# A four-layer graph network on one core: layer 0's weight products from 7 block products instead of 8, with a planner that prefers open PSUM banks

## The chip, the cores and the metric

The kernel runs on one core of a Trainium2 chip. Its engines are TensorE (PE in the profile, with its weight loads as PEld), VectorE (DVE), ScalarE (ACT), GpSimd (POOL) and SyncE (SP), which here only issues DMA transfers. The metric is the device time of one execution in microseconds (us); shorter is better. A profiled execution also has a span, from its first to its last instruction, which is a little shorter than its device time.

## What is computed

`x` is (64, 256, 128): 64 batches, 256 nodes, 128 channels. `adj` is (256, 256). Everything is fp32. Cut to what matters:

```python
def layernorm(x, eps=1e-5):                       # over the 128 channels, no gain, no bias
    return (x - mean(x)) / sqrt(var(x) + eps)

# layer 0: six propagations, adj twice, three powers each; seven 128x128 weights
xs = [x, A@x, A@A@x, A@A@A@x, A@x, A@A@x, A@A@A@x]
x = layernorm(x + sum(xs[k] @ W[:, :, k] for k in range(7)))
# layer 1
x = layernorm(x + A @ (x @ w1) + b1)
# layer 2: Ahat = A + I, scaled by its row sums d**-0.5 on both sides
x = layernorm(x + (Anorm @ x) @ W2.T + b2)
# layer 3: five steps of a gated unit
h = x
for _ in range(5):
    av = concat(A @ h, A @ h)
    u3 = h @ u3_w.T + u3_b
    z = sigmoid(av @ w3_w.T + w3_b + u3)
    r = sigmoid(av @ w4_w.T + w4_b + u3)
    hv = tanh(av @ w5_w.T + w5_b + (r * h) @ u5_w.T + u5_b)
    h = (1 - z) * h + z * hv
x = layernorm(x + h)
```

In layer 0 the two adjacencies are the same, so equal powers share one weight: with `w0s[0] = W0 + I` (the residual) and `w0s[k] = Wk + W(k+3)`, and with each weight's mean over the output channels taken off so that the result is already centred, the layer is `x w_0 + A x w_1 + q w_2 + A q w_3`, where `q = A A x`. The kernel forms `s = (x w_0 + q w_2) + A (x w_1 + q w_3)`.

## The kernel before

**Groups.** The batches go two at a time (`NB` = 2), which makes 32 groups. A group's data is a tile of 128 partitions by 512 columns: two batches, two halves of the 256 nodes, 128 channels. Each group goes through the four layers; up to `ACTIVE` = 10 groups are under way at once (`gate`, `load_gate`).

**Planner.** Nothing is issued as it is written. Each group records its steps (`Group.record`) as operations with an engine, a planned cost, a lag after it, the values it reads and writes, and a rank (the group's number; for the last 7 groups compressed so that they advance together). `Plan.order` (L84) then lays all operations out by list scheduling: at each turn it takes, for each engine, the operation that could start first, and among those of equal start the one of lowest rank and then of lowest record number (L117). A value gets a buffer ("slot") when its first operation is placed and gives it back after its last user; the eight PSUM banks are such slots. The order that comes out is the program: each engine executes its own list in that order, and a semaphore holds an instruction until what it needs is there.

**Products by seven blocks.** `Group.seven` (L593) multiplies a 256x256 adjacency with a group's data as a 2x2 block matrix in the manner of Strassen and Winograd: 7 products of 128x128 blocks, with sums of blocks made on POOL (`ts01`, `ts2`, `ts3`) and put together on ACT and DVE. Its PE work is four operations: `first` (1 block product, L626), `middle` (3, which need the sums, L629), `more` (1, L634) and `rest` (2, L637). `more` overwrites a part of the bank that ACT must have copied before (`kept`, L655), and `rest` overwrites parts that the DVE operations `post12` and `post13` must have read.

**Layer 0.** For groups from the fifth batch on ("far" groups, 30 of 32) `x` is turned by a DVE transpose of 32x32 blocks, a DMA write to memory and two DMA reads (L745 to L755); its channels arrive in an order of their own, so the kernel holds a copy of two weights permuted to match (`w0p`, made by four DMAs, L308). `q` comes from `seven`. Then, for each node half `t`, four matmuls 128 to 256 columns wide make `x [w_0 w_1]` and `q [w_2 w_3]` side by side into one bank (`first`, L764, tiles `py`), ACT copies the right half out as `v` (L771), two matmuls per half add `A v` to the left half (`second`, L777), and ACT copies the sum out as `s0` (L783). Two banks are held for it.

**Layer norm.** `spread_of` (L509): four ACT squares with a running sum (L515) leave the variances in `ve`; POOL adds eps (L519) and takes the power -1/2 (L520).

**Start and end.** Constants are loaded and prepared first, with ranks that place them among the first groups' work: `p_an`, the transposes of the normalised adjacency (L259, L344), which need `ahat` scaled by DVE (L334); `p_w2u3T` and `p_w435u5T`, the turned weights of layers 2 and 3 (L391). The last three groups (`END` = 6 batches) end in `closing` (L557), which turns `h` back and centres it on PE; the others go back through a transpose and DMAs.

The line of every matmul in the profile is that of the helper `mm` (L199), so they are told apart by their tiles: `py` weight products and layer 0, `pm` and `pmq` and `pmg` the block products of layers 1 and 2, of `q`, and of layer 3, `pr` and `ph` the gates. An fp32 matmul or weight load shows as two instructions.

## Time and profile before

| what | value |
|---|---|
| device time, median of 4 runs | 1353.43 us (1350.84 to 1355.65) |
| the profiled execution: device time | 1350.84 us |
| the profiled execution: span | 1348.9 us |
| mean granted TensorE clock | 0.999 |
| ACT busy | 758.1 us, 56% of the span |
| POOL busy | 680.7 us, 50% |
| DMA engines, mean busy share of the main queue | 34.1% |

The profiled execution was the fastest of the four; 1.9 us of its time lie outside the span. A row of the profile's groups names the source line, the engine, the operation, the tiles written and read, the shape and the count, then the busy time and the mean duration of one; a row of the timeline gives the start and the duration in us. Matmuls are pipelined, so that a matmul's duration in such a row is longer than the distance to the next one's start; it is the distance between starts that says what a matmul costs PE.

### The profile page before, as it was taken

The page shows a single profiled execution, that of the slowest core. Times are in us where ns is not written, and L with a number is a line of the kernel's source. Part 1 is how long each engine was busy: PE and PEld are TensorE (multiplying, and loading weights), DVE is VectorE, ACT ScalarE, POOL GpSimd, SP SyncE. Part 2 cuts the span into 40 slices and gives each one's busy share as a digit, 9 for nine tenths or more (in the row PEclk, how much of TensorE's full clock was granted, in tenths as well). Part 3 has the DMA queues.
Part 4 walks back from the last instruction along what each step waited for, and adds up shares of the span by engine and source line. Part 5 has one row for each costly group of instructions (what it writes and reads, how often), then busy time and mean ns, then how long its engine had stood idle before and what let it go on. Part 6 is the DMA issues. An engine that isn't in the chain of part 4 may idle for free.

```text
span 1348.9 us, 22012 instructions
## 1 busy us (share of the span) xinstructions
PE 1335.8 (99%) x6553; PEld 927.7 (69%) x6553; DVE 940.2 (70%) x2304; ACT 758.1 (56%) x2421; POOL 680.7 (50%) x1097
## 2 busy tenths in 40 slices
PE   8999999999999999999999999999999999999997
PEld 7986656677766666677666666676776776565554
DVE  5466677767667667865676776676666677777776
ACT  4675536467554566546565554474655686444445
POOL 5885425276742566247366443382653686233323
PEclk9999999999999999999999999999999999999999
DMA  6322334242422333433233433341332223333323
GB/s 180 107 69 80 90 93 129 75 130 87 134 78 79 109 95 118 122 103 96 63 113 107 133 98 97 95 134 56 113 99 63 83 85 122 86 104 95 95 77 110
DMA packets 269496, 134.96 MB, mean 100 GB/s; under 512 B 175777, under 2 KB 241057, under 8 KB 269377
## 3 DMA queue, kind: packets, MB, share of 16 engines
q1 hardware_dynamic: 269120, 133.42, 34.1%
q8 instruction: 53, 0.87, 0.3%
q14 instruction: 67, 0.54, 0.1%
q0 software_dynamic: 256, 0.13, 0.1%
HBM read 67.31 MB, written 65.80 MB: 99 GB/s over the span
## 4 chain that ended last, share of the span: by engine, by line
PE 97%; DMA 1%; DVE 1%; ACT 1%; issue 0%; POOLq 0%; SPq 0%; ACTq 0%; POOL 0%; DVEq 0%
PE pr L199 31%; PE ph L199 20%; PE pmg L199 19%; PE py L199 16%; PE pm L199 7%; PE pmq L199 4%; DMA w_raw<-in_L_gnn_weight_dram 0%; PE s L199 0%; DMA x<-in_x_dram 0%; ACT y L515 0%; ACT y L551 0%; DVE s L543 0%; POOLq L908 0%; DVE w0s L289 0%; PE p_an L259 0%
## 5 line engine op out<-in xcount | busy, mean ns | idle before, releaser
L199 PE MATMUL pr<-mg,w435u5T 128*128 128x512 f32 x640 | 319.8, 593 | 0.0
L614 POOL TENSOR_TENSOR tsg<-h 128x256 f32<-128x256 f32 x128 | 96.9, 758 | 291.0 <-DMA h<-dh 207.6
L722 ACT ACTIVATE r<-pr,bsum 128x512 f32<-128x512 f32 x160 | 109.7, 685 | 152.2 <-PE pr L199 151.7
L722 ACT ACTIVATE pr<-pr,bsum 128x512 f32<-128x512 f32 x160 | 105.5, 660 | 112.4 <-PE pr L199 111.4
L729 DVE TENSOR_TENSOR rh<-r,hT 128x512 f32<-128x512 f32 x160 | 122.4, 765 | 61.8 <-ACT r L722 60.9
L199 PE MATMUL ph<-rh,w435u5T 128*128 128x512 f32 x320 | 163.6, 594 | 0.0
L199 PE MATMUL ph<-mg,w435u5T 128*128 128x512 f32 x320 | 163.3, 592 | 0.0
L199 PE MATMUL pr<-hT,w2u3T 128*128 128x512 f32 x320 | 163.0, 593 | 0.0
L729 DVE TENSOR_TENSOR d<-ph,hT 128x512 f32<-128x512 f32 x160 | 109.7, 686 | 76.3 <-ACT ph L722 73.4
L199 PEld LDWEIGHTS pr<-mg,w435u5T 128*128 128x128 f32 x640 | 109.4, 191 | 65.3 <-issue 53.8
L722 ACT ACTIVATE ph<-ph,bsum 128x512 f32<-128x512 f32 x160 | 105.6, 660 | 60.4 <-PE ph L199 59.9
L531 ACT ACTIVATE y<-s,rs 128x128 f32<-128x128 f32 x384 | 122.1, 393 | 10.3 <-POOL rs L520 10.0
L515 ACT ACTIVATE y<-s 128x128 f32<-128x128 f32 x396 | 116.7, 300 | 17.1 <-DVE s L538 15.1
L199 PEld LDWEIGHTS pmg<-s_aTp,tsg 128*128 128x128 f32 x768 | 101.8, 192 | 33.5 <-issue 29.6
L652 DVE TENSOR_TENSOR mg<-pmg,usg 128x256 f32<-128x256 f32 x160 | 67.0, 420 | 72.1 <-PE pmg L199 69.8
L199 PEld LDWEIGHTS pmg<-aTp,h 128*128 128x128 f32 x512 | 87.1, 197 | 39.4 <-issue 29.2
L729 DVE TENSOR_TENSOR pr<-pr,d 128x512 f32<-128x512 f32 x157 | 108.7, 692 | 1.5
L520 POOL TENSOR_TENSOR rs<-ve,half 128x4 f32<-128x4 f32 x99 | 103.6, 1046 | 8.3
L519 POOL TENSOR_SCALAR ve<-ve 128x4 f32<-128x4 f32 x99 | 23.7, 240 | 165.6 <-ACT y L515 165.2
L729 DVE TENSOR_TENSOR hT<-hT,pr 128x512 f32<-128x512 f32 x157 | 106.1, 676 | 1.3
L199 PE MATMUL pmg<-s_aTp,tsg 128*128 128x128 f32 x768 | 106.2, 275 | 0.0
L642 DVE TENSOR_TENSOR usg<-usg,pmg 128x128 f32<-128x128 f32 x160 | 45.2, 284 | 83.2 <-PE pmg L199 48.0
(181 smaller groups left out, 2815.7 us busy)
## 6 DMA issues: line engine op xcount, KB each, us to landing
dh<-th SPq DMA_DIRECT2D x160, 256.0 KB, 2.0
h<-dh SPq DMA_DIRECT2D x256, 128.0 KB, 2.5
x<-in_x_dram SPq DMA_DIRECT2D x32, 256.0 KB, 3.4
hT<-dh SPq DMA_DIRECT2D x128, 64.0 KB, 2.0
out_dram<-y SPq DMA_DIRECT2D x32, 256.0 KB, 2.3
dx<-tx SPq DMA_DIRECT2D x30, 256.0 KB, 2.4
xT<-dx SPq DMA_DIRECT2D x60, 128.0 KB, 2.6
dn<-tn SPq DMA_DIRECT2D x29, 256.0 KB, 2.0
```

The lines of the kernel that those rows point to most:

```text
L199: nc.tensor.matmul(o, lhsT, rhs, start=start, stop=stop, skip_group_check=shared)
L515: nc.scalar.activation(nat(y)[:, q, :], nat(s)[:, q, :], AF.Square, scale=C ** -0.5, accum_out=ve.ap[:, q:q + 1])
L519: nc.gpsimd.tensor_scalar(ve.ap, ve.ap, EPS, None, op0=OP.add)
L520: nc.gpsimd.tensor_tensor(rs.ap, ve.ap, half[:, :self.q], op=OP.pow)
L531: nc.scalar.mul(nat(y)[:, q, :], nat(s)[:, q, :], rs.ap[:, q:q + 1])
L614: nc.gpsimd.tensor_tensor(ts.ap[:, :2 * P].rearrange("p (x c) -> p x c", x=2), ins(h)[:, 1], ins(h)[:, :, 0], op=OP.subtract)
L642: nc.vector.tensor_tensor(row(u, 0), row(u, 1), row(ps, 3), op=OP.add)
L652: nc.vector.tensor_tensor(o(m, slice(1, 3)), o(ps, slice(1, 3), False), both, op=OP.add)
L722: self.act(lambda: nc.scalar.activation(t.ap, ps.ap, func, bias=bias[1], scale=1.0), [ps, bias[0]], [t], act_cost(self.width) + 100)
L729: self.dve(lambda: nc.vector.tensor_tensor(out(t), way(a), way(b), op=op), [a, b], [t])
```

## The change

Four things change.

1. **The planner's key.** Among operations of one engine that could start at the same time, one that uses a bank already taken (`opens` = 0) now goes ahead of one that does not, whatever their ranks.
2. **Layer 0 of the far groups** is recorded by a new function, `inner_seven`, which makes the four products with the weights as a 2x2 block product with 7 block products: sums of weights (`w0t`, made once on DVE), sums of the data on DVE (`s1` to `s4`), 14 matmuls of 128 columns, and five additions on DVE that put the results together. The two groups of the first four batches keep the old form, moved to `inner`. The transpose of `x` now reads its columns in a pattern that brings the channels in their natural order, so `w0p` and its four DMAs go. A new kind of half-width buffer, `h`, holds the sums.
3. **`seven`**: `first` and `middle` become one operation `opening` of 4 block products, recorded after the POOL sums.
4. **Layer norm's eps**: the squares get a bias of sqrt(eps/C) per partition (`root`), which adds eps to the sum because the data is centred; POOL's addition of eps goes.

The ranks of two constants (`rows`, `p_an`) also move from 0.3 to 0.9 and 1.1, and `rows` now also waits for `w0s`.

```diff
@@ Plan.order
-                    need = {}
+                    need, opens = {}, 1
                     for v in placed[op]:
                         if v.slot is None:
                             need[v.kind] = need.get(v.kind, 0) + 1
+                        elif v.kind == "bank":
+                            opens = 0
...
-                    key = (max(at, t0), op.rank, op.seq)
+                    key = (max(at, t0), opens, op.rank, op.seq)
@@ constants
+    root = const.tile([P, 1], F32, name="root")
+    nc.vector.memset(root, (EPS / C) ** 0.5)
...
-    w0p = constant("w0p", [P, 2, C])
-    def permuted():
-        for r in range(4):
-            nc.sync.dma_start(w0p.ap.rearrange("(j r) k c -> r j k c", r=4)[r], w0s.ap[32 * r:32 * (r + 1), 0:2, :])
-    pre(1.2, "SP", 1800, permuted, [w0s], [w0p])
+    w0t = constant("w0t", [P, 4, C])
+    def w0_blocks():
+        w_0, w_1, w_2, w_3 = (w0s.ap[:, k, :] for k in range(4))
+        t1, t2, t3, t4 = (w0t.ap[:, k, :] for k in range(4))
+        nc.vector.tensor_sub(t1, w_1, w_0)
+        nc.vector.tensor_sub(t2, w_3, t1)
+        nc.vector.tensor_sub(t3, w_3, w_1)
+        nc.vector.tensor_sub(t4, w_2, t2)
+    pre(1.2, "DVE", 1000, w0_blocks, [w0s], [w0t])
...
-    pre(0.3, "DVE", 600, rows, [ahat, dinv], [ahat])
-    pre(0.3, "PE", 4 * 110, lambda: turn(p_an, ahat), [ahat], [p_an])
+    pre(0.9, "DVE", 600, rows, [ahat, dinv, w0s], [ahat])
+    pre(1.1, "PE", 4 * 110, lambda: turn(p_an, ahat), [ahat], [p_an])
@@ spread_of
                     nc.scalar.activation(nat(y)[:, q, :], nat(s)[:, q, :], AF.Square, scale=C ** -0.5,
-                                         accum_out=ve.ap[:, q:q + 1])
+                                         bias=root[:, 0:1], accum_out=ve.ap[:, q:q + 1])
             def scales():
-                nc.gpsimd.tensor_scalar(ve.ap, ve.ap, EPS, None, op0=OP.add)
                 nc.gpsimd.tensor_tensor(rs.ap, ve.ap, half[:, :self.q], op=OP.pow)
@@ new: inner_seven, the core
+            def s3(): nc.vector.tensor_tensor(whole(sd), at(xT, 0), at(xT, 1), op=OP.subtract)
+            def s1(): nc.vector.tensor_tensor(whole(ss), at(xT, 1), at(qT, 1), op=OP.add)
+            def s2(): nc.vector.tensor_tensor(whole(st_), whole(ss), at(xT, 0), op=OP.subtract)
+            def s4(): nc.vector.tensor_tensor(whole(sf), at(qT, 0), whole(st_), op=OP.subtract)
+            def times(o, a, w, start=False):
+                for b in range(NB):
+                    mm(o[:, b], a[:, b], w, start and b == 0, True, shared=True)
...
+            def both():
+                times(half(more, 0), whole(st_), w0t.ap[:, 1, :], True)
+                times(half(more, 1), whole(ss), w0t.ap[:, 0, :])
...
+            self.pe(pe_cost(P, NB), lambda: times(half(out_, 0), at(xT, 0), w0s.ap[:, 0, :], True), [xT, w0s], [out_])
+            self.act(lambda: nc.scalar.copy(u1.ap, out_.ap[:, :N]), [out_], [u1], 270)
+            self.pe(pe_cost(P, 2 * NB), both, [ss, st_, w0t], [more])
+            self.pe(pe_cost(P, NB), lambda: times(half(out_, 0), at(qT, 0), w0s.ap[:, 2, :]), [qT, w0s], [out_])
+            self.pe(pe_cost(P, NB), lambda: times(half(out_, 1), at(qT, 1), w0t.ap[:, 3, :]), [qT, w0t], [out_])
+            add(lambda: (u2.ap, u1.ap, more.ap[:, :N]), [u1, more], [u2])
+            self.pe(pe_cost(P, NB), lambda: times(half(more, 0), whole(sd), w0t.ap[:, 2, :]), [sd, w0t], [more])
+            add(lambda: (u3.ap, u1.ap, more.ap[:, :N]), [u1, more], [u3])
+            add(lambda: (half(v, 1), whole(u3), half(more, 1)), [u3, more], [v])
+            self.pe(pe_cost(P, NB), lambda: times(half(more, 1), whole(sf), w0s.ap[:, 3, :]), [sf, w0s], [more])
+            add(lambda: (half(v, 0), whole(u2), half(more, 1)), [u2, more], [v], True)
+            for t in range(T):
+                def second(t=t):
+                    for kt in range(T):
+                        mm(half(out_, t), aT.ap[:, kt, t * P:(t + 1) * P], half(v, kt), False, True, shared=True)
+                self.pe(pe_cost(N, T), second, [v, aT], [out_])
+            self.act(lambda: nc.scalar.copy(s0_t(0), half(out_, 0)), [out_], [s0], 270)
+            add(lambda: (s0_t(1), whole(u3), half(out_, 1)), [u3, out_], [s0], True)
@@ seven
-            def first():
+            def opening():
                 block(0, ins(h)[:, 0, 0], aTs.ap[:, 0, :P], True)
-            def middle():
                 block(2, row(ts, 0), sums.ap[:, 0, :])
...
-            started = self.pe(pe_cost(P, 1), first, [h, aTs], [ps])
-            kept = self.act(lambda: nc.scalar.copy(row(u, 1), row(ps, 0)), [ps], [u], 165)
             self.add("POOL", 830, 100, ts01, [h], [ts])
             self.add("POOL", 610, 100, ts2, [h, ts], [ts])
             self.add("POOL", 590, 100, ts3, [h, ts], [tq])
-            self.pe(pe_cost(P, 3), middle, [ts, sums], [ps], True, (started,))
+            self.pe(pe_cost(P, 4), opening, [h, ts, aTs, sums], [ps])
+            kept = self.act(lambda: nc.scalar.copy(row(u, 1), row(ps, 0)), [ps], [u], 165)
             self.pe(pe_cost(P, 1), more, [h, aTs], [ps], True, (kept,))
@@ record, far groups
-                    x_.ap.rearrange("p (b t r j) -> p r b t j", r=4, t=T, j=32)), [x_], [turn])
+                    x_.ap.rearrange("p (b t j r) -> p r b t j", r=4, t=T, j=32)), [x_], [turn], 1000)
...
-            v, s0 = self.val("w", "v"), self.val("w", "s0")
...
+            s0 = (self.inner if near else self.inner_seven)(xT, qT)
```

## The prediction

> **What bounds the kernel now.** I read the busy times and the chain first, then the busy time by stretches, then the timeline of PE in the steady part, at the start and at the end.
>
> ```profile
> PE 1335.8 (99%) x6553; PEld 927.7 (69%) x6553; DVE 940.2 (70%) x2304; ACT 758.1 (56%) x2421; POOL 680.7 (50%) x1097
> PE 97%; DMA 1%; DVE 1%; ACT 1%; issue 0%; POOLq 0%; SPq 0%; ACTq 0%; POOL 0%; DVEq 0%
> ...
> 60.00:1340.00 1280.00, 1278.33 (x6209) 875.93 (x6208) 907.35 (x2213) 722.66 (x2277) 639.16 (x1025) 1.00 0.34 98
> ```
>
> The first line is the page's busy part, the second its chain that ended last, the third the busy time by stretch (PE, PEld, DVE, ACT, POOL, then PE clock, DMA share, GB/s). From 60 to 1340 us PE idles 1.7 us of 1280 at a granted clock of 1.00. No other engine is above 71% there, and no wait of theirs is worth anything unless it makes PE late. So the kernel is PE work, plus about 60 us of start and 9 us of end. The question is what the change does to PE's work, and how much new idleness it puts between.
>
> What one matmul costs PE is the distance between starts:
>
> ```profile
> 605.21 0.60 PE L199 MATMUL py<-w0p,xT 128*128 128x256 f32 x2
> ...
> 606.94 1.05 PE L199 MATMUL py<-w2u3T,m 128*128 128x128 f32 x8
> 607.83 0.38 PE L199 MATMUL py<-v,aT 128*128 128x256 f32 x1
> 616.39 0.40 PE L199 MATMUL pmg<-aTp,h 128*128 128x128 f32 x2
> 616.63 0.40 PE L199 MATMUL pmg<-s_aTp,h 128*128 128x128 f32 x2
> ```
>
> From 605.21 to 606.94 lie four matmuls of 256 columns (one node half of layer 0): 1.73 us, 0.433 each. From 606.94 to 607.83 lie four of 128 columns, each with its own weights: 0.89 us, 0.223 each. One whose weights are read with a stride (`h` by pairs) takes 616.63 - 616.39 = 0.24. So 128 columns cost half of 256, to within 3%.
>
> **The weight products.** A far group has 8 matmuls of 256 columns now: 2 x 1.73 = 3.46 us. After it has 14 of 128: 12 x 0.223 + 2 strided (`xT` by pairs) x 0.24 = 3.16 us. `second` keeps its four matmuls of 256 columns. Saved: 0.30 us x 30 groups = **-9.0 us** of PE work, all on the path. Against this speaks a rule of the Trainium skill ("TensorE: Matmul & The Clock Gate", section "Back-to-back issue gap"): in a stream of weight load and matmul pairs the load takes part in the spacing, so that 128-wide matmuls come 81 ns apart and not 55.6. By that ratio, an estimate, a half-width matmul would cost 0.217 x 1.46 = 0.32 us, the 14 of them 4.4 us, and the edit would lose some 29 us. The row of four 128-wide matmuls above, each with its own load, shows 0.223, so the sum goes by the row.
>
> **What it adds to DVE, ACT and POOL.** Durations of one, by their groups:
>
> ```profile
> L652 DVE TENSOR_TENSOR mg<-pmg,usg 128x256 f32<-128x256 f32 x160 | 67.0, 420 | 72.1 <-PE pmg L199 69.8 <-ACT y L531 1.2
> L543 DVE TENSOR_TENSOR s<-hn,y 128x512 f32<-128x512 f32 x29 | 21.8, 753 | 0.0
> L383 DVE TENSOR_TENSOR both_w<-raw_w 128x128 f32<-128x128 f32 x3 | 0.7, 282 | 0.0
> L515 ACT ACTIVATE y<-s 128x128 f32<-128x128 f32 x396 | 116.7, 300 | 17.1 <-DVE s L538 15.1 <-PE s L199 1.3
> L531 ACT ACTIVATE y<-s,rs 128x128 f32<-128x128 f32 x384 | 122.1, 393 | 10.3 <-POOL rs L520 10.0
> ```
>
> The five additions from PSUM are 256 wide: 0.42 each. The four sums read SBUF twice; at 256 they lie between 0.28 (128 wide) and 0.75 (512 wide), I take 0.44. Per group 5 x 0.42 + 4 x 0.44 = 3.9 us, x 30 = 116 us, so DVE goes to about 1057 us, 79%. ACT loses 60 copies of 0.371 (two of four per far group): -22 us; the squares' bias becomes an operand read per partition, and 300 to 393 ns is what a row without and one with such an operand show, so +0 to 396 x 0.093 = 37 us. POOL loses 99 x 0.24 = 24 us. The new transpose pattern has no row; bounds are nothing and one more transpose, 0.70 us x 30, on DVE. All of this lies beside PE, at a price of 0 while PE's next work is ready; without that cover it is paid as lateness, below. Dropping `w0p` takes four issues (2.4 us) from SP's queue; nobody waited there.
>
> **Order.** I compared the order of instructions of both kernels. Two effects of the planner's key and of `opening` show. Banks are held far shorter: measured in PE work between a bank's first and last matmul, `pmq` 30 us before, 7 after, `pmg` 8.3 and 5.9. And dependent steps move together. `more` must wait for ACT's copy of what `first` (now `opening`) left; between them stood a median 3.7 us of other PE work, under 1.0 us in 25 of 254 places; after, 1.3 us, under 1.0 in 101. What such a chain needs when it fails:
>
> ```profile
> 697.96 0.39 PE L199 MATMUL pm<-aT,y 128*128 128x128 f32 x2
> 698.70 0.94 PE L199 MATMUL pm<-s_aT,ts 128*128 128x128 f32 x6 [0.35 <-ACT us L655]
> ```
>
> The copy's chain took 698.70 - 697.96 - 0.22 = 0.52 us with nothing between, so 1.0 us holds if ACT is free, and not if a gate (0.66) or four squares (1.2) stand ahead in ACT's queue. Counting the places where one operation ahead in the same queue uses the cover up, over all chains of one step: about 120 before, 173 after. Before, the starts of PE's matmuls show some 10 stalls after 60 us, about 5 us together: one in 12 places. At that rate 53 more places give 4 more stalls of 0.5 us: **+2.2 us**. Bounds: 0, if the shorter bank times remove as many; +17, if a third of the 101 fail. I take the known rate.
>
> **Start.** Today PE waits here:
>
> ```profile
> 7.54 0.60 PE L674 MATMUL ptx<-ident,x 128*128 128x128 f32 x4
> 9.62 0.81 PE L259 MATMUL p_an<-ident,ahat 128*128 128x128 f32 x4 [1.48 <-DVE ahat L334]
> 10.26 0.60 PE L674 MATMUL ptx<-ident,x 128*128 128x128 f32 x4
> 10.70 2.32 PE L199 MATMUL pmq<-a2T,x 128*128 128x256 f32 x10
> ...
> L229 SPq DMA_DIRECT2D raw_u<-in_L_gnn_u_w_dram x2: 328/379/430, 6.4 to 8.0; - x2
> DMA to landing us min/median/max: 4.2/4.7/5.1
> ```
>
> `p_an` moves back behind the first groups' products, so that wait goes; but in the new order `p_w2u3T` stands ahead of `pmq`, and it needs `raw_u3`, issued at 6.4 and landing 4.2 to 5.1 us later, at 10.6 to 11.5. With it (0.2 us) `pmq` starts at 10.8 to 11.7, not 10.70; behind it queue both first groups. Take +1.0. Later, PE's waits between 27 and 40 us (1.3 us shown for `pmq`, a few tenths more) are re-dealt: the far groups' `xT` lands near 27 us as before and is now needed from 27, not 30, while DVE has 5 sums of `anT` and a transpose ahead of the first combination. I take -0.5, together **+0.5**, bounds -1 and +4.
>
> **End.** The last matmuls keep their set. But DVE's order now has four statistics of group 56 (25.0 us / 116 = 0.22 each) between `d` and `e` of the last group. `s<-e` follows 2.64 us of PE work after `ph`; the chain is 0.26 + 0.66 (tanh) + 0.69 + 0.69 = 2.3, with the statistics 3.2: PE late by 0.5. On POOL `rs` of group 56 (1.04 and 0.23) goes ahead of the last `rs`: +0.9. The eps addition gone: -0.3. Together **+1.0**, bounds -0.3 and +1.5.
>
> **Sum.** -9.0 + 2.2 + 0.5 + 1.0 = -5.3 us. On the profiled execution: 1350.84 - 5.3 = 1345.5. It was 2.6 us under the median of the four runs; on that, 1353.43 - 5.3 = **1348.1**, taken as 1348.
>
> **Rivals.** *The whole saving shows.* The new stalls stay away because banks are free: ends at their low bounds give -9.0 + 0 - 1 - 0.3 = -10.3, 1343. For it: the steady part loses 1.7 us in 1280 today with tight places already there. Against: the order of start and end. *The saving is eaten.* About 10 more stalls at 0.5, a start at +2 and the end at +1: -9.0 + 8 = -1, 1352. For it: DVE's 116 us more, in stretches where it is 78% busy already. *Slower, by `more`:* PE executes in order, so each late copy stops everything behind `more`. From 26 stalls on (-9.0 + 1.5 + 0.5 x 26 = +5.5) the kernel is slower; if 45 of the 101 close places fail it is at -9.0 + 1.5 + 22.5 = +15, 1368. For it: ACT's gates and normalisations come in blocks of 0.7 to 1.6 us. Against: in the steady part ACT is idle 44% and often waits for PE at these very copies (25.2 us for `usg`). *That it does not do what it says* is out: the order shows 14 matmuls of 128 columns in each far group.
>
> **Chances.** Forecast 0.45, whole saving 0.17, eaten 0.22, slower 0.16. 0.3% is 4.06 us, about what a measurement of this kernel tells from no change. The first two are faster by more, except for the forecast's slow edge: faster 0.61, same 0.23, slower 0.16. The range 1342 to 1356 goes from the full saving less a microsecond of spread to the eaten case with a few more stalls, and leaves out most of the slower case. The likeliest case alone is 1344 to 1350.
>
> **What would show it.** Right: `py` of 128 columns start 0.22 us apart and PE's busy time falls by about 9; idleness of PE from 60 to 1340 us at 3 to 5 us; `pmq` first at 11 to 12 us; the last stretch 1 us longer. Wrong: a wait of PE for ACT at L767 that sums to 10 us, 128-wide matmuls 0.3 us apart, or DVE naming PE's waits.

## The result, and the profile after

The changed kernel takes 1356.07 us (median of 33 runs, 1354.31 to 1361.19), the kernel before on the same chips 1354.72 us (median of 53, 1350.84 to 1356.77). The ratio is 1.0012, 95% interval [1.0007, 1.0017]: about 1.4 us more, where 5.3 less were forecast. Two facts about the base come with it. The 1350.84 us that the sum was made against is the fastest of all 53 runs of before. And a second profile of before (the run *e1* below, 1354.79 us, at the median) shows why: the first 25 us differ, the rest does not.

The page of the changed kernel, its busy times and the chain that ended last:

```profile
PE 1332.5 (98%) x6913; PEld 931.3 (69%) x6913; DVE 1055.3 (78%) x2579; ACT 774.0 (57%) x2361; POOL 662.5 (49%) x998
PE 87%; DVE 6%; ACT 3%; DMA 2%; issue 1%; POOL 1%; SPq 0%; POOLq 0%; DVEq 0%; ACTq 0%
```

PE is busy 3.3 us less than the 1335.8 of before although the span grew by 5.9 us (1348.9 to 1354.8). The chain of before was 97% PE; here 10% of it runs through DVE, ACT and POOL. So PE has less to do and waits more.

Its busy time by stretches (stretch, length, then busy PE, PEld, DVE, ACT, POOL with counts, granted PE clock, DMA share, GB/s):

```profile
8.00:12.00 4.00, 1.11 (x9) 0.81 (x8) 1.11 (x4) 1.07 (x2) 1.32 (x3) 1.00 0.72 202
12.00:16.00 4.00, 2.70 (x11) 2.03 (x10) 3.69 (x14) 0.96 (x2) 0.00 (x0) 0.72 0.42 102
16.00:20.00 4.00, 4.00 (x17) 3.42 (x16) 3.97 (x13) 1.17 (x2) 2.42 (x5) 0.85 0.40 119
...
60.00:1330.00 1270.00, 1263.84 (x6513) 873.41 (x6513) 996.71 (x2425) 733.99 (x2220) 620.54 (x933) 1.00 0.34 97
```

The same stretch of before:

```profile
60.00:1330.00 1270.00, 1268.33 (x6163) 869.63 (x6162) 899.75 (x2185) 716.19 (x2255) 635.02 (x1019) 1.00 0.34 97
```

From 60 to 1330 us PE idles 6.2 us in the changed kernel and 1.7 in before. At the start PE idles 4.2 us between 8 and 16 us, and its clock is granted at 0.72 and 0.85 behind that.

What PE waits for in the changed kernel, in all, times, longest:

```profile
PE ptx L782 <- DMA x<-in_x_dram: 2.9, 1, 2.9
PE ph L201 <- DVE rh L837: 2.5, 4, 1.2
...
PE p_w2u3T L408 <- DMA raw_u<-in_L_gnn_u_w_dram: 1.3, 1, 1.3
PE pmq L201 <- DVE mq L757: 1.2, 2, 0.7
PE pmq L201 <- ACT usq L767: 1.1, 1, 1.1
PE pz L201 <- DVE se L622: 0.8, 1, 0.8
PE pm L201 <- ACT us L767: 0.8, 1, 0.8
```

The `raw_u` wait is the one forecast for the start. Behind it DVE names most of the waits, and L767, ACT's copy ahead of `more`, sums to 1.9 us only.

These waits are long enough to be named, but most lost time is in smaller steps. So I counted PE in another way: the distance between one matmul's start and the next's, less the time that a matmul of its kind needs, the median step of that kind in the same trace (0.112 us for a pass of 128 columns, 0.117 or 0.118 where its weights are read with a stride, 0.216 for 256, 0.429 for 512; two passes to an fp32 matmul). What is left over are PE's *stalls*; a step that is long because the clock was low counts too. The columns of this table add up to the span, with 1.36 us ahead of PE's first matmul:

| profile | span | PE's issue time | stalls, first 25 us | stalls, after 25 us | from PE's last start to the end |
|---|---|---|---|---|---|
| before, first profile | 1348.9 | 1329.9 | 3.8 | 6.7 | 7.1 |
| before, second profile (e1) | 1352.8 | 1329.9 | 7.6 | 6.9 | 7.1 |
| changed | 1354.8 | 1320.4 | 9.0 | 15.4 | 8.7 |

Against the second profile of before: -9.5 of issue time, +1.4 at the start, +8.5 after 25 us, +1.5 at the end, together +1.9 after rounding, where the spans differ by 2.0. The medians are whole nanoseconds, and one nanosecond on the strided passes moves up to 0.8 us between the columns of issue time and stalls: at one price for both kernels, issue time falls by 8.9 us and the stalls after 25 us grow by 8.0. PE's saving came in full. It went into stalls spread over the whole run, and those after 25 us are the question.

By what stalls (over 0.1 us each, after 25 us, in brackets the second profile of before): `more` 4.8 us at 21 steps (0.5 at 4, `first` taken in), `ph` 4.4 at 14 (0.3 at 3), the first product of `rest` 3.8 at 13 (3.8 at 6), the new bank `pz` 1.6 at 3 (none), and the products of `middle`, now part of `opening`, none (1.2 at 6). One row each of `more` and of `rest`:

```profile
L201 PE MATMUL pmq<-a2T,x 128*128 128x128 f32 x120 | 22.4, 278 | 1.2 <-ACT usq L767 1.1
L201 PE MATMUL pmq<-s_a2T,x 128*128 128x128 f32 x60 | 11.8, 278 | 1.2 <-DVE mq L757 1.2
```

`more` reads the adjacency itself (`a2T`) and waits for ACT's copy (L767); the first row also counts the first product of `opening`, at which no such stall lies. `rest` reads the sums of its blocks (`s_a2T`) with the data, and waits for DVE's `post13` (L757).

### The profile page after: what moved, and what is told of

Read it like the earlier page. It is cut to its first block, busy times and chain, and to the rows that moved or that the text cites. A ratio compares the mean times of both kernels' runs of the same rounds, so it can differ in the third digit from the quotient of the medians.

```text
span 1354.8 us, 22575 instructions
## 1 busy us (share of the span) xinstructions
PE 1332.5 (98%) x6913; PEld 931.3 (69%) x6913; DVE 1055.3 (78%) x2579; ACT 774.0 (57%) x2361; POOL 662.5 (49%) x998
## 4 chain that ended last, share of the span: by engine, by line
PE 87%; DVE 6%; ACT 3%; DMA 2%; issue 1%; POOL 1%; SPq 0%; POOLq 0%; DVEq 0%; ACTq 0%
PE pr L201 29%; PE ph L201 20%; PE pmg L201 17%; PE py L201 9%; PE pm L201 6%; PE pz L201 4%; PE pmq L201 2%; ACT y L524 2%; ACT y L539 1%; DMA raw_w<-in_L_gnn_w_w_dram 1%; DVE ss L619 1%; DVE rh L837 0%; DVE tx L851 0%; DVE se L622 0%; DMA x<-in_x_dram 0%
## 5 line engine op out<-in xcount | busy, mean ns | idle before, releaser
L528 POOL TENSOR_TENSOR rs<-ve,half 128x4 f32<-128x4 f32 x99 | 100.8, 1019 | 189.1 <-ACT y L524 182.3
L524 ACT ACTIVATE y<-s,root 128x128 f32<-128x128 f32 x396 | 153.7, 392 | 37.3 <-DVE s L546 32.5
L201 PEld LDWEIGHTS pmg<-aTp,h 128*128 128x128 f32 x512 | 90.5, 196 | 67.9 <-issue 37.8
L871 POOL TENSOR_TENSOR yb<-y,wb 128x512 f32<-128x512 f32 x64 | 83.4, 1303 | 37.2 <-ACT y L539 35.4
L201 PE MATMUL pmg<-aTp,h 128*128 128x128 f32 x512 | 99.4, 280 | 0.1
L201 PEld LDWEIGHTS ph<-rh,w435u5T 128*128 128x128 f32 x320 | 57.0, 190 | 59.3 <-issue 38.2
L510 POOL TENSOR_TENSOR rs<-ve,half 128x4 f32<-128x4 f32 x29 | 30.3, 1045 | 135.0 <-DVE nm L507 134.8
```

What stands on the lines that cost most here:

```text
L201: nc.tensor.matmul(o, lhsT, rhs, start=start, stop=stop, skip_group_check=shared)
L510: nc.gpsimd.tensor_tensor(rs.ap, ve.ap, half[:, :self.q], op=OP.pow)
L524: nc.scalar.activation(nat(y)[:, q, :], nat(s)[:, q, :], AF.Square, scale=C ** -0.5, bias=root[:, 0:1], accum_out=ve.ap[:, q:q + 1])
L528: nc.gpsimd.tensor_tensor(rs.ap, ve.ap, half[:, :self.q], op=OP.pow)
L871: nc.gpsimd.tensor_tensor(nat(yb), nat(y), bias[1][:, None, :].to_broadcast([P, self.q, C]), op=OP.add)
```

## The experiments

"Same order" marks runs in which every engine's queue is in the order of the changed kernel, so that only the edited instructions differ. In the other runs the edit touches a planned cost, a rank or a dependence, and the planner draws another order almost everywhere. Stalls are those after 25 us in the run's profile. In a few runs the clock also fell to half for some microseconds after 25 us (e2, e3, e6 with the opening split, e7, e14, e18), and their stalls hold that too: 1.7 us of the 14.9 in e18.

| run | median us | ratio to before [95%] | stalls |
|---|---|---|---|
| e1 before again | 1354.79 (one) | | 6.9 |
| e2 sums issued on POOL, same order | 1367.5 | 1.0100 [1.0087, 1.0114] | 27.0 |
| e3 sums planned on POOL | 1375.23 | 1.0155 [1.0141, 1.0169] | 35.4 |
| e4 old key | 1366.5 | 1.0090 [1.0077, 1.0104] | 27.1 |
| e5 eps on POOL | 1352.3 | 0.9984 [0.9975, 0.9993] | 11.6 |
| e6 opening split | 1360.14 | 1.0039 [1.0027, 1.0051] | 19.1 |
| e7 block products alone | 1358.93 | 1.0031 [1.0021, 1.0041] | 23.5 |
| e8 start reordered | 1353.46 | 0.9994 [0.9985, 1.0003] | 15.8 |
| e9 = e5 + e8 | 1347.78 | 0.9955 [0.9942, 0.9967] | 9.9 |
| e12 sums left out, same order | 1347.27 | 0.9953 [0.9940, 0.9965] | 7.7 |
| e13 sums formed, not read, same order | 1355.81 | 1.0015 [1.0007, 1.0024] | 15.7 |
| e6 sums planned at 600 | 1352.02 | 0.9980 [0.9971, 0.9989] | 11.4 |
| e11 squares planned at 390 | 1347.99 | 0.9947 [0.9933, 0.9960] | 8.6 |
| e16 eps on POOL, same order | 1355.28 | 1.0004 [0.9995, 1.0012] | 12.6 |
| e15 control, sums planned at 350 | 1351.09 | 0.9966 [0.9954, 0.9979] | 9.4 |
| e14 = e9 + sums planned at 600 | 1351.32 | 0.9972 [0.9963, 0.9982] | 13.4 |
| e17 before, copies +10 ns | 1363.38 | 1.0078 [1.0063, 1.0094] | 16.5 |
| e18 before, scales +10 ns | 1362.05 | 1.0063 [1.0050, 1.0077] | 14.9 |

### First round: one part undone at a time

**The kernel before, once more.** No edit.

> The kernel before, unchanged, for a second profile. The first profiled execution (1350.84 us) was the fastest of 53, 3.9 under their median of 1354.72, so the two traces compared exaggerate what the change lost. If its luck was in the start (in it the third load landed 6.3 us after its issue, x of group 2 by 10.3 us), PE's first pmq product here starts at 12 us or later and idleness from 60 to 1340 us stays under 3 us. If the luck was in the steady part, the start is the same as before and PE idles 3 us or more after 60 us.

Its span is 1352.8, 3.9 us longer than the first profile's, and 3.8 of these lie in the first 25 us: PE waits 3.9 us for `ahat` instead of 1.5. After 25 us the stalls are 6.9 and 6.7 us. So the sum was made against an execution that was lucky at its start, and the steady part repeats from run to run.

**The sums on POOL**, in the order of the changed kernel, then planned there.

```diff
-                nc.vector.tensor_tensor(whole(ss), at(xT, 1), at(qT, 1), op=OP.add)
+                nc.gpsimd.tensor_tensor(whole(ss), at(xT, 1), at(qT, 1), op=OP.add)
...
-            self.add("DVE", 340, 260, s1, [xT, qT], [ss])
+            self.add("POOL", 830, 100, s1, [xT, qT], [ss])
```

All four sums alike; the last two lines are in the second run only.

> The changed kernel with the four sums s1 to s4 executed by GpSimd, while the planner still plans them on DVE, so that every other engine keeps its order. Theory S: the four sums, which read SBUF twice and take up to 1.48 us instead of 0.42 while GpSimd works, make DVE late and through it PE; off DVE the stalls of PE for DVE (rh, se, v: about 6 of the 8 us of new steady stalls) go, and the kernel takes 1350 us or less. Theory K (the planner's key puts dependent steps too close): DVE's load is not the point, 1354 to 1358 us. Against both: GpSimd, with 4 x 30 sums of about 0.75 us that its plan does not know of, becomes late itself, and the kernel takes over 1358 us.

> As the run before, but the planner knows that the sums are GpSimd's (planned at 830 ns), so the order is laid out for it. Theory S: the gain of the run before and more, 1346 to 1350 us. Theory K: 1353 to 1358 us.

Both are far slower than the changed kernel, by 11 and 19 us. DVE's load falls, but the sums come later, and with them the block products: in the first of the two PE waits once 5.0 us at `pz` for the `u` that DVE can't form. The theory that moving the sums off DVE helps fell. It does not say that DVE's load is harmless, since the work went to a slower engine; that is told apart in the second round.

**The old key.**

```diff
-                    key = (max(at, t0), opens, op.rank, op.seq)
+                    key = (max(at, t0), op.rank, op.seq)
```

> The changed kernel with the planner's old key (start, rank, record number): everything else of the change stays. Theory K: PE's idleness from 60 to 1340 us falls from 6 us to about 2, and the time is 1347 to 1350 us. Theory S: the sums stay on DVE and stretch as before, the time is 1353 to 1358 us; more banks are held, and it may be slower still.

10 us slower than the changed kernel, with stalls of 27.1. The theory that the key costs the time fell; how much the key is worth is one draw of an order (see the third round).

**eps on POOL again**, without the bias operand.

```diff
-                                         bias=root[:, 0:1], accum_out=ve.ap[:, q:q + 1])
+                                         accum_out=ve.ap[:, q:q + 1])
+                nc.gpsimd.tensor_scalar(ve.ap, ve.ap, EPS, None, op0=OP.add)
-            self.add("POOL", 1040, 100, scales, [ve], [rs])
+            self.add("POOL", 1330, 100, scales, [ve], [ve, rs])
```

> The changed kernel with eps back as GpSimd's addition and no bias in the squares. Theory E (the bias operand makes each square 392 ns instead of 300, 0.39 us from start to start instead of 0.30, a group of four 1.57 us instead of 1.2, which its planned 1.18 us does not tell; ACT is late and PE with it): ACT's busy time falls by 30 us or more, the stalls of PE after 60 us fall from 12 to 7 us or less, and the time is 1348 to 1352 us. If the bias is hidden: 1355 to 1358 us.

3.8 us faster than the changed kernel. At this point I read it as the price of the bias operand; the runs on order below took that back.

**The opening split again**: A's first product ahead of ACT's copy, the three others behind, as in the kernel before.

```diff
-            self.pe(pe_cost(P, 4), opening, [h, ts, aTs, sums], [ps])
-            kept = self.act(lambda: nc.scalar.copy(row(u, 1), row(ps, 0)), [ps], [u], 165)
+            started = self.pe(pe_cost(P, 1), first, [h, aTs], [ps])
+            kept = self.act(lambda: nc.scalar.copy(row(u, 1), row(ps, 0)), [ps], [u], 165)
...
+            self.pe(pe_cost(P, 3), middle, [ts, sums], [ps], True, (started,))
```

> The changed kernel with the first four block products split again into one and three. Theory O (the products in one go leave too little work between them and the next, which waits for ACT's copy): the time falls to 1348 to 1352 us. If the joint opening is what keeps the banks short: 1360 us or more, as with the old key.

**The block products alone**: the kernel before with `inner_seven`, `w0t` and the new transpose, but with the old key, the split opening, eps on POOL and the old ranks.

```diff
-            qT = self.propagate("q", x_, a2T, fast=not near)
...
+            qT = self.propagate("q", x_, a2T, fast=not near)
+            s0 = (self.inner if near else self.inner_seven)(xT, qT)
```

> The kernel before with the 7 block products of layer 0 alone: old key, first block product apart, eps on GpSimd, old ranks of the start. The saving of 9.4 us in PE's work is in it. If the stalls come with DVE's added work, whatever the order: 1354 us or more. If they come from the other three parts: 1345 to 1349 us.

4.1 and 2.9 us slower than the changed kernel. In the second PE's issue time is 1321.0, so the block products save their 9 us by themselves, and in this order 23.5 us of stalls take more than that away (some 3.6 of them are steps at half clock, from 30.7 and from 494.9 us on). Both are single orders, so neither difference is the price of its edit.

**The start reordered**: group 2's transposes on PE behind the first `pmq`, and `p_w2u3T` told to wait for `w0s`.

```diff
-        pre(2.1, "PE", len(parts_) * 110, run, [*parts_, less], [ps])
+        pre(2.1, "PE", len(parts_) * 110, run, [*parts_, less, w0s], [ps])
...
-            self.pe(pe_cost(P, self.q) / 2, run, [src], [ps])
+            self.pe(pe_cost(P, self.q) / 2, run, [src], [ps], behind=[o for o in pmq_first if self.start])
```

> The changed kernel with two edges added at the start: the transposes of group 2's x come after the first pmq product, and the turned weights of layers 2 and 3 after w0s. It takes away PE's waits for x of group 2 and for raw_u3 (2.9 and 1.3 us in the profile of the changed kernel) and with them the loss of the clock at 14 us (1.7 us). If these are worth what the profile shows, PE's first pmq product starts at 10 us or earlier, and the time is 1350 to 1353 us; if later waits take their place, 1354 to 1358 us.

2.6 us faster than the changed kernel. Its stalls after 25 us are the same (15.8 and 15.4), those of the first 25 us are 5.6 instead of 9.0. Here the place is shown, not only the sum: the wait for `raw_u` is gone, that for `x` is 0.7 us instead of 2.9, a new one of 1.8 us for `w0s` comes in, and the clock stays at 1.00.

### Second round: is it DVE's load?

The two parts that gave something, together:

> The changed kernel with two of its costs undone together: eps added on POOL again (no bias operand on ACT's squares) and the start reordered (group 2's transposes behind the first pmq, p_w2u3T behind W0). Alone they gave 3.8 us (1356.1 to 1352.3) and 2.6 us (to 1353.5). Theory A, that they are separate sums (ACT's 0.09 us a square over the whole span, and waits of the first 20 us): 1349 to 1350.5, below both kernels, with about 9 us of PE's idle time after 100 us and 10 in the first 100. Rival B, that each is only a reshuffle of the plan's order and the stalls come back elsewhere: 1352 to 1355.

1347.78 us, 8.3 under the changed kernel and 6.5 under before on the same chips. It is more than the two gains together, which was the first sign that something else moved with the edits.

**The sums left out, and the sums formed but not read**, both in the same order. In the first, each sum of the 30 far groups is a write of one column, and the products that read the sums read A; in the second the sums are formed and the products still read A. That part of layer 0 is so not computed in either.

```diff
-                nc.vector.tensor_tensor(whole(ss), at(xT, 1), at(qT, 1), op=OP.add)
+                nc.vector.memset(ss.ap[:, :1], 0.0)
...
-                times(half(more, 1), whole(ss), w0t.ap[:, 0, :])
+                times(half(more, 1), aT.ap, w0t.ap[:, 0, :])
```

> The changed kernel with its plan and the order of its instructions as they are, but the four sums of each of the 30 far groups are left out (each becomes a write of one column, so that buffers and waits stay), and the four pairs of products that read them read the constant A instead; the part of layer 0 that goes through the sums is so not computed. PE's work is the same. Theory D, that the stalls after 100 us (12.2 us against 5.6 before the change) are DVE running late under 30 x 4 more operations (78 us): DVE falls from 1055 to about 985 us, the stalls to 6 to 8 us, the time to 1350 to 1352. Theory W, that PE waits for the sums themselves (pz waits for se): the same time, but then the next run gains as much. Theory O, that it is the new chain of block products, copies and adds with its two banks: 1354 to 1357, no gain.

> As the run before, but the four sums are formed as in the changed kernel, and only the products read the constant A in their place (the same part of layer 0 is not computed). DVE has all its work, PE waits for none of the sums. Theory D (DVE's load): 1354.5 to 1357, stalls after 100 us 11 to 13 us, as in the changed kernel. Theory W (the waits for the sums): as the run before, 1350 to 1352. The trace names a sum in waits of about 1 us in all, so W should be worth no more than that.

This pair tells the theories apart. Without the sums: 1347.27 us, 8.8 under the changed kernel and below the 1350 to 1352 of theory D, stalls 7.7 instead of 15.4. With the sums formed and nobody reading them: 1355.81, as the changed kernel, stalls 15.7. So PE doesn't lose its time in waiting for the sums. It loses it because DVE is busy with them and is late with everything else: stalls at `ph`, which waits for DVE's `rh`, are 4.4 us in the changed kernel and with the unread sums, 1.1 without sums; at `rest`, which waits for DVE's `post13`, 4.7 with the unread sums and 2.0 without; at `more` 4.8 and 3.4. PE's busy time from 60 to 1330 us says the same, first with the sums left out, then formed and not read:

```profile
60.00:1330.00 1270.00, 1267.98 (x6528) 876.07 (x6527) 956.16 (x2442) 736.23 (x2226) 611.65 (x935) 1.00 0.34 98
```

```profile
60.00:1330.00 1270.00, 1264.20 (x6516) 873.79 (x6515) 996.81 (x2421) 733.68 (x2225) 621.43 (x934) 1.00 0.34 97
```

2.0 us idle and 5.8, with the same matmuls. Over the whole span DVE is busy 1001.5 us instead of 1056.0. POOL, with the same 998 instructions, is busy 651.2 instead of 662.7: the two engines slow each other.

**The sums planned at what they take.**

```diff
-            self.add("DVE", 340, 260, s1, [xT, qT], [ss])
+            self.add("DVE", 600, 260, s1, [xT, qT], [ss])
```

> The changed kernel with the sums' planned cost on DVE set from 340 to 600 ns, near what the trace shows of them under POOL's work (mean 0.63 to 0.71 us; 0.42 without). Nothing else changes than the order that the plan draws from it. Theory D in its form 'the plan does not know how long DVE is busy': the plan spreads DVE's work better, stalls after 100 us 7 to 10 us, 1351 to 1354. Rival, that the loss is a matter of DVE's real load and stretches that no order avoids: 1355 to 1358.

4.0 us faster, as the theory had it. Whether that is the truer cost or just another order was not to be told from this run alone.

### Third round: is it the edit, or the order that comes with it?

> The changed kernel, bias operand kept, with the squares' planned cost on ACT set from 295 to 390 ns each, what the trace shows of them. Theory P, that the 3.8 us which undoing the bias gave came from the plan not knowing ACT's true time: 1351 to 1353.5, stalls after 60 us 8 to 10 us in place of 12.4. Theory E, that it came from ACT's longer work itself, whatever the plan knows: 1355 to 1357.5.

> The changed kernel with its plan kept, so that every engine's order is that of the changed kernel, and only the instructions differ: the squares without the bias operand, the add of eps issued on POOL again. Theory E (ACT's 0.09 us a square, some 32 us over the span, makes PE's operands late in this order): 1351 to 1354. Theory P or order alone: 1355.5 to 1357.5, no gain.

> A control. The changed kernel with the sums' planned cost on DVE 350 in place of 340 ns: no instruction differs, but the plan draws another order nearly everywhere. If the order alone is worth little: 1355 to 1357. If a small nudge of the plan moves the time by 3 us or more to either side, then the gains of the runs that changed the plan (3.8 us with eps on POOL, 4.0 with the sums planned at 600) cannot be put down to their edits by themselves, and only the runs that keep the order (sums left out, sums formed and not read) tell a cause.

> The run of eps on POOL with the start reordered (1347.8) with the sums planned at 600 ns too. Theory A (the true cost helps the plan in any order): 1343.5 to 1346. Rival B (that gain belonged to one order): 1346.5 to 1350.

Their edits, in this order:

```diff
-            self.act(squares, [s], [y, ve], 295 * self.q)
+            self.act(squares, [s], [y, ve], 390 * self.q)
...
-                                         bias=root[:, 0:1], accum_out=ve.ap[:, q:q + 1])
+                                         accum_out=ve.ap[:, q:q + 1])
+                nc.gpsimd.tensor_scalar(ve.ap, ve.ap, EPS, None, op0=OP.add)
...
-            self.add("DVE", 340, 260, s1, [xT, qT], [ss])
+            self.add("DVE", 350, 260, s1, [xT, qT], [ss])
```

and the last is the combined run of the second round with the sums planned at 600.

The control decides. Ten nanoseconds in one planned cost, with no instruction changed, make the kernel 5.0 us faster. Its stretch from 60 to 1330 us:

```profile
60.00:1330.00 1270.00, 1268.08 (x6545) 876.64 (x6544) 1005.45 (x2440) 736.89 (x2230) 622.85 (x936) 1.00 0.34 98
```

1.9 us idle instead of 6.2, at 8.7 us *more* of DVE's busy time in the stretch. So DVE's load costs what the pair showed in the order of the changed kernel, and little in this one: that order is a poor draw among near neighbours.

The bias operand does lengthen ACT's work. Squares of one node group in the changed kernel, then in the same order without the bias:

```profile
252.31 0.39 ACT L524 ACTIVATE y<-s,root 128x128 f32<-128x128 f32 x1
252.60 0.19 ACT L524 ACTIVATION_READ_ACCUMULATOR y<-s,root 128x1 f32 x1
252.69 0.39 ACT L524 ACTIVATE y<-s,root 128x128 f32<-128x128 f32 x1
```

```profile
252.15 0.30 ACT L524 ACTIVATE y<-s 128x128 f32<-128x128 f32 x1
252.35 0.19 ACT L524 ACTIVATION_READ_ACCUMULATOR y<-s 128x1 f32 x1
252.45 0.29 ACT L524 ACTIVATE y<-s 128x128 f32<-128x128 f32 x1
```

Starts are 0.38 and 0.30 apart. But in the same order undoing it gives 1355.28 against 1356.07, and the intervals of the two ratios ([0.9995, 1.0012] and [1.0007, 1.0017]) overlap, so any gain is not clear of noise. What the run with eps on POOL gained, and even more the one with the squares planned at 390 (8.1 us, with the bias kept, below the ranges of both its theories), cannot be put down to the operand. Adding the truer cost of the sums to the best run made it 3.5 us slower. 1351.32 lies above the ranges of both theories; it falls on the rival's side, a truer planned cost does not help in every order. The fastest of all are so two kernels of the changed kernel's instructions or nearly so, 1347.78 and 1347.99 us, both below before and changed.

**Two other orders of the kernel before.**

```diff
-                self.act(moved, [p], [v], 55 + 107 * self.nb)
+                self.act(moved, [p], [v], 65 + 107 * self.nb)
...
-                self.act(summed, [py[t]], [s0], 55 + 107 * self.nb)
+                self.act(summed, [py[t]], [s0], 65 + 107 * self.nb)
```

and, in the other run, only this:

```diff
-            self.add("POOL", 1330, 100, scales, [ve], [ve, rs])
+            self.add("POOL", 1340, 100, scales, [ve], [ve, rs])
```

> A control for the kernel before: two planned costs on ACT (the copies of v and s0 in layer 0) raised by 10 ns, no instruction differs, the plan's order does nearly everywhere. Four plans of the changed kernel that do the same work as it gave 1356.1 (its own), 1351.1 (sums 350), 1352.0 (sums 600) and 1348.0 (squares 390). If the order of before is one draw among many like it, this gives 1351 to 1358, to either side of 1354.7. If the order of before is a good draw that the change lost, 1357 to 1363, and the seven block products are worth that much more than the comparison shows. If orders of before all lie alike, 1354 to 1355.5.

> A second draw for the kernel before: the planned cost on POOL of the eps add and the power raised from 1330 to 1340 ns, no instruction differs. The same three cases: 1351 to 1358 (one draw among many), 1357 to 1363 (before is a good draw), 1354 to 1355.5 (its orders lie alike).

1363.38 and 1362.05 us: the second case, before is a good draw (the first of them is 0.4 us above its range). The stretch from 60 to 1330 us of the first of them:

```profile
60.00:1330.00 1270.00, 1263.21 (x6139) 866.83 (x6138) 888.96 (x2164) 712.76 (x2254) 631.60 (x1018) 1.00 0.33 97
```

6.8 us idle, where the kernel before has 1.7. Its stalls after 25 us are 16.5 and, in the other run, 14.9, as many as the changed kernel has. The 6.7 us of the kernel before belong to its own order.

So both kernels of this comparison are draws. Orders measured with before's instructions: 1354.7, 1362.1, 1363.4, mean 1360.1. With the changed kernel's instructions and only planned costs moved: 1348.0, 1351.1, 1352.0, 1356.1, mean 1351.8. The difference of the means is -8.3 us. With three draws against four, 8 us apart within each kernel, this is an estimate without an interval. Two of the four (1348.0 and 1352.0) also set a planned cost nearer to its true time, so they are not blind draws; the other two alone, mean 1353.6, would leave -6.5. But the best of before is beaten by three of the four. Of the changed kernel the worst of the four was compared with the best of the three.

## Why the prediction was wrong, point by point

**Weight products, -9.0: right, measured -8.9 to -9.5.** The new products' starts:

```profile
624.49 0.61 PE L201 MATMUL pz<-w0t,se 128*128 128x128 f32 x4
624.94 0.61 PE L201 MATMUL pz<-w0t,ss 128*128 128x128 f32 x4
```

Two matmuls (four passes) in 0.45 us, 0.225 each, as the row of before had it.

**DVE, ACT and POOL: right in size, for DVE partly by luck, and the price of 0 is where the trouble starts.** DVE was put at 1057 us and has 1055. Two of the sums' groups in the changed kernel, one of the additions from PSUM, and the transpose with the new pattern:

```profile
L644 DVE TENSOR_TENSOR v<-u,pz 128x256 f32<-128x256 f32 x60 | 24.7, 412 | 4.5 <-PE pz L201 4.2
...
L619 DVE TENSOR_TENSOR ss<-xT,mq 128x256 f32<-128x256 f32 x30 | 19.0, 634 | 0.1
L625 DVE TENSOR_TENSOR sf<-mq,se 128x256 f32<-128x256 f32 x30 | 17.4, 578 | 0.2
...
L851 DVE STREAM_TRANSPOSE tx<-x 128x512 f32<-128x512 f32 x30 | 33.0, 1102 | 3.3 <-DMA x<-in_x_dram 3.3
```

The additions cost 0.41, as taken. The sums cost 0.56 to 0.63, not 0.44, and the transpose 1.10 instead of 0.70. The durations of DVE's instructions add up to 143 us more than before; its busy time grew by only 115 because they overlap one another more. ACT's 774 us are the upper end of what was allowed for: the squares' bias costs its full 0.09 each. The prediction said of all this work that without cover it "is paid as lateness, below", and below there was no term for it: the only chain counted was the one through ACT's copy and `more`. The pair of runs with the sums left out and unread puts 8.5 us on the sums alone, in this order.

**Order, +2.2: this is the step that failed, and with it the price of 0 for DVE's added work.** It measured +8.0 to +8.5, and PE idles 6.2 us from 60 to 1340 us where 3 to 5 were to show the forecast right. It was sized by a rate, 10 stalls in 120 tight places, "one in 12", read in the profile of before and carried to the new order. The rate was a property of one order and not of the kernel: before's instructions in two other orders stall 16.5 and 14.9 us. The place that it named was right, the size too low: at `more` the stalls are 4.8 us where before had 0.5, or 1.7 together with `middle` (the row with which the prediction prices a failed chain is one of `middle`, it reads `ts`). The larger part lies where the sum had no term: `ph` +4.1 and `pz` +1.6, behind a DVE that is 78% busy, as the same-order pair shows. The bounds, 0 to +17, held the value; the rate picked from them did not.

**Start, +0.5: low by 0.9 against the second profile of before**, within its bounds. The wait for `raw_u` came as worked out, 1.3 us. Not foreseen was the wait of 2.9 us for `x`, which with the other put the first `pmq` at 14.2 us and not at 11 to 12, nor that PE's clock falls there (below). In the second profile of before `pmq` starts at 13.9 us and the clock falls too; the start that the term was worked out from was the lucky one.

**End, +1.0: low.** The tail grew by 1.5 us, and two stalls at `s`, for DVE's `e` behind the statistics of group 56, add 0.5. The chain was the one described.

**The base.** The sum was also applied to the median of four, 1353.43, which further runs moved to 1354.72.

With 8.5 in place of 2.2 alone, the sum becomes -9.0 + 8.5 + 0.5 + 1.0 = +1.0, close to the +1.4 measured. The rival "saving eaten" had the right size (a gain of about nothing) and the right cause in its "for it" (DVE's 116 us), but was priced in stalls of `more` too. "Slower, by `more`" had the place, not the size: 4.8 us of stalls there in all, where its price began at 13. Of the signs of being wrong, DVE naming PE's waits came; L767 summed to 1.9 us, not 10.

Open: why the order of before is good, that of the changed kernel poor, in terms that could be read from the orders without running them; and whether truer planned costs help on the average, for which one run each is not enough.

## What to carry to other kernels

Where a planner draws the order, run the kernel before and the changed one in several orders each, by nudging a planned cost by some nanoseconds, before a difference of a few microseconds is put down to an edit; to find the cause of a stall, edit only the instructions and keep the order. A stall rate read in one order is no property of the kernel. Work added to an engine that is three quarters busy and feeds the bound engine needs a term of its own, even where no wait names it.

## What the runs showed of the hardware

**DVE and POOL slow each other.** DVE operations with two operands in SBUF stretch while POOL works. The clearest place in the changed kernel:

```profile
270.21 1.26 POOL L871 TENSOR_TENSOR yb<-y,wb 128x512 f32<-128x512 f32 x1 [1.29 <-ACT y L539]
270.24 1.78 DVE L837 TENSOR_TENSOR rh<-r,hT 128x512 f32<-128x512 f32 x1
...
271.43 1.18 POOL L725 TENSOR_TENSOR ts<-y 128x256 f32<-128x256 f32 x1
...
272.07 1.12 PE L201 MATMUL ph<-rh,w435u5T 128*128 128x512 f32 x2 [1.17 <-DVE rh L837]
```

`rh` takes 1.78 us under two POOL operations, and PE waits 1.17 for it. The 72 of the 160 `rh` that no POOL instruction overlaps have a mean of 0.684 us, the other 88 one of 0.803. `d`, of the same width but with an operand in PSUM, has 0.686 and 0.685. The Trainium skill has the reason in a line ("GPSIMD Engine Reference", section "Specifications"): GpSimd shares its SBUF interfaces with VectorE and contends with VectorE's instructions of two SBUF inputs. These rows agree: `rh` stretches and `d` does not.

**PE's clock falls behind waits at the start.** Between 12 and 20 us the changed kernel's clock was 0.72 and 0.85 (stretches above), behind waits of 2.9 us for `x` and 1.3 for `raw_u`. In the run with the sums left out, with the same instructions up to there, `x` landed sooner and the waits were 1.9 and 1.3 us:

```profile
8.00:12.00 4.00, 1.85 (x12) 1.22 (x10) 1.85 (x7) 1.66 (x3) 1.20 (x3) 1.00 0.67 193
12.00:16.00 4.00, 3.01 (x15) 2.68 (x16) 3.90 (x16) 0.96 (x2) 0.00 (x0) 1.00 0.56 159
16.00:20.00 4.00, 4.00 (x20) 3.54 (x19) 3.90 (x10) 0.96 (x2) 3.23 (x6) 1.00 0.12 34
```

There the clock stays at 1.00. With the sums formed and not read the wait for `x` was 3.8 us, and the clock from 12 to 16 us was 0.50:

```profile
12.00:16.00 4.00, 3.08 (x11) 2.51 (x11) 3.62 (x14) 0.96 (x2) 0.00 (x0) 0.50 0.38 100
```

At the low clock of the changed kernel seven passes of 256 columns took 0.427 us each from start to start in place of 0.216, 1.5 us in all, on top of the waits. The Trainium skill's "TensorE: Matmul & The Clock Gate", section "What's actually happening", puts the fall to half clock after about 3.4 us of idleness. The 3.8 us with a fall and 1.9 without agree with that; the changed kernel's fall, with no single wait above 2.9 us, agrees only in kind. And in the run with the block products alone the clock fell at 494.9 us, behind 3.4 us in which PE was busy for 1.95 and no wait was longer than 0.65: here the measurement differs from an unbroken idle time of 3.4 us. What sets the fall is not shown.

**ACT's per-partition bias isn't hidden here.** With the accumulator read between, squares with a bias operand start 0.38 to 0.40 us apart, without it 0.29 to 0.30; so a group of four takes some 0.36 us longer.
